# Gating by token block, earlier shared additions and a halved last store in a two-layer transformer kernel

## The chip, the cores and the metric

The kernel runs on one core of a Trainium2 chip, all in 32-bit floats. The metric is the time of one execution on the device in microseconds (us), taken several times; one more execution is recorded by the profiler.

## The reference

Two layers, each of attention and a feed-forward network, on x of shape (2, 512, 1024) and a context of (2, 1024, 1024):

```python
x = x + matmul(fake_quant(layernorm(x)), fake_quant(ctx))        # quantised product
x = x + lora_ffn(layernorm(x))        # x @ W.T + b + 8 routed LoRA experts, routing per batch
x = x + cross_attention(layernorm(x), ctx, ctx)   # 32 heads of 128, 8 key/value heads, rope
x = x + top1_ffn(layernorm(x))        # the end of the kernel, in full:

def _L1_ffn_ref(x, W_up, gate_w, expert_bias, lora_A, lora_B):
    logits = x_flat @ gate_w.T + expert_bias          # 4 experts
    top1 = jnp.argmax(logits, axis=-1)
    one_hot = jax.nn.one_hot(top1, E)
    base_out = jnp.einsum('bth,oh->bto', x, W_up)
    z = jnp.einsum('nh,erh->ner', x_flat, lora_A)     # rank 8
    d = jnp.einsum('ner,ehr->neh', z, lora_B) * SCALE
    delta = jnp.einsum('neh,ne->nh', d, one_hot)
    return base_out + delta.reshape(B, T, H)
```

## The kernel before

**Tiles.** Tokens lie in four blocks (t = 0 to 3) of 128 per batch; `rows(b, t)` is one of them, 128x1024, in SBUF. A map of 1024 to 1024 over 512 tokens is done as a product of 2x2 blocks with seven products instead of eight. `linear(b, ...)` (L562) is such a map; it works in two halves, `blocks(0)` and `blocks(1)`, woven by `pair`. `blocks(s)` gives the token blocks s and 2 + s. Each of the seven products is 16 or 20 TensorE instructions of 128x512 (L347, four or five pairs, each 32-bit product as four instructions) into a bank of PSUM.

**The seven products.** `seven_onto` (L304) adds their results onto rows that are already there. In `linear` their order is 1, 2, 6, 7, 5, 4, 3. Product 1 is copied by ScalarE into `u` (L315); product 6 is added to `u` by VectorE (L317): this is the shared sum. Each other product is added by VectorE onto its quarter `c` of the rows (L320), and for the products 5, 4 and 3 GpSimd then adds `u` onto that quarter (L322). Products 7 and 4 share a bank, as do 1 and 2, and 5 and 3: the second is accumulated onto the first. The output projection of the attention uses `seven_onto` with its own order. `linear` is called for the first network of both batches (L1076) and for the last network of both batches (L1203 and L1238), which is the end of the kernel.

**The gates.** `gated` is the choice of the expert in the last network. It makes, for each token block, 16 TensorE instructions (L937; eight fp32 products of 128x36: 4 logits and 4 x 8 ranks) into one PSUM tile `gaccs` of four parts. Then, for each block, seven VectorE operations choose the expert: bias (L949), maximum (L951), equality (L953), a preference for the first (L954), maximum (L955), equality (L956), and the product of the chosen expert's mask with the ranks, out of PSUM into `z` (L961). Two blocks share a tile `z2`, which GpSimd sets to zero first (L959). TensorE transposes each block's `z` (L971), VectorE copies the result to `zT` (L972) and takes a difference (`split_tokens`). `zT` is the LoRA operand of the final map.

**The order.** `gated` is a generator; whoever calls `next` places its parts. For batch 0 this happens in the attention's loop, where TensorE, VectorE, ScalarE and GpSimd all keep the order in which the program names their instructions. `hooks` maps (head, phase) to calls: at (61, 2) `begin_map` creates the generator; at (62, 1) `advance(last["gates"], 4)` issues the products of all four blocks; at (62, 2) the VectorE and GpSimd operations follow; at (63, 1) the transposes, and the final map begins. Around them stand the sums of the attention's denominators (four transposes L712, a reduction L714, a reciprocal L785), the exponentials of the last head (L794 on VectorE, L797 on ScalarE, L800, L803, L804 and L805 on GpSimd), the last product of a head with its values (L811), and the normalisation L822 on GpSimd.

For batch 1 `turned_and_gated` is woven with the final map of batch 0: one step of it after each product. Each step turns a block of normalised rows (L204, copies L205 and L206) and issues a block's gate products. TensorE keeps the order of the program there too; on the other engines a scheduler sets the order.

**The end.** The rows of batch 1 are stored by four transfers of 512 KB on SyncE's queue (L1244); the last map's products 4 and 3 write the last quarters.

Of the kernel before, what the change touches and what calls it, by code (L numbers as in the profile page):

```python
# [15 lines left out]
ALU = mybir.AluOpType  # L16
AX = mybir.AxisListType

P = 128
# [5 lines left out]
E1, R1 = 4, 8  # L25
# [6 lines left out]
NT = S // P  # L32
NC = D // P
NKT = S2 // P
HALF = 512
# [4 lines left out]
def decoder_kernel(  # L40
# [25 lines left out]
    nc = tc.nc  # L66
# [8 lines left out]
    def new(shape, tag, bufs, dtype=F32):  # L75
        n_tiles[0] += 1
        return sb.tile(list(shape), dtype, tag=tag, name=f"{tag}_{n_tiles[0]}", bufs=bufs)
# [7 lines left out]
    def u2(shape, dtype=F32):  # L85
        return new(shape, "u2", 10, dtype)

    def small(shape):
        return new(shape, "small", 16)

    def ps_wide():
        n_tiles[0] += 1
        return ps.tile([P, D], F32, tag="wide", name=f"wide_{n_tiles[0]}", bufs=2)

    def ps_b(shape=(P, HALF), dtype=F32):
        n_tiles[0] += 1
        return ps.tile(list(shape), dtype, tag="b", name=f"b_{n_tiles[0]}", bufs=4)

    def ps_tr():
        return ps_b((P, 4, P))  # L100
# [16 lines left out]
    for name, ap in qparams.items():  # L117
        t = const.tile([P, 1], F32, name=f"qp_{name}")
        nc.gpsimd.dma_start(t, ap.partition_broadcast(P))
        qp[name] = t  # L120
    for side in ("x1", "x2"):
        t = const.tile([P, 1], F32, name=f"qp_inv_{side}")
# [21 lines left out]
    NGA = E1 + E1 * R1  # L144
# [156 lines left out]
                emit(0, 1, u)  # L301
            yield

    def seven_onto(product, place, order=(1, 6, 2, 7, 5, 4, 3)):  # L304

        banks = {}
        for i in order:
            first = {2: 1, 4: 7, 3: 5}.get(i, i)
            if i == first:
                banks[i] = ps_b()  # L310
            acc = banks[first]
            product(i, acc, i == first)
            if i == 1:
                u = u2([P, HALF])
                nc.scalar.copy(u, acc)  # L315
            elif i == 6:
                nc.vector.tensor_tensor(u, u, acc, ALU.add)  # L317
            else:
                c = place(*{2: (0, 0), 7: (1, 1), 5: (1, 1), 4: (1, 0), 3: (0, 1)}[i])
                nc.vector.tensor_tensor(c, c, acc, ALU.add)  # L320
                if i != 2 and i != 7:
                    nc.gpsimd.tensor_tensor(c, c, u, ALU.add)  # L322
            yield

    def pair(a, b):

        for _ in range(2):
            next(a)
            yield
            next(b)  # L330
            yield
        yield from a
        yield from b
# [11 lines left out]
    def accumulate(acc, pairs, start):  # L345
        for k, (lhsT, rhs) in enumerate(pairs):
            nc.tensor.matmul(  # L347
                acc,
                lhsT,
                rhs,  # L350
                start=start and k == 0,
                stop=k == len(pairs) - 1,
                skip_group_check=True,
            )
# [16 lines left out]
    def rows(b, t):  # L371
        return x[b][t // 2][:, t % 2, :]
# [168 lines left out]
    def chunk(quarters, c, t):  # L541
        return quarters[t // 2][c // 4][:, c % 4, ts(t % 2, P)]
# [19 lines left out]
    def linear(b, h_ops, w_ops, tT, bl):  # L562

        def blocks(s):
            lora = {2: (0, 0), 4: (1, 0), 5: (1, 1), 3: (2, 1)}

            def product(i, acc, start):
                pairs = [
                    (h_ops[i - 1][:, c, ts(s, P)], w_ops(i, c))
                    for c in range(4)  # L570
                ]
                if i in lora:
                    th, nh = lora[i]
                    pairs.append((tT()[th][:, ts(s, P)], bl[:, ts(nh, HALF)]))
                accumulate(acc, pairs, start)

            return seven_onto(
                product,
                lambda i, j: rows(b, 2 * i + s)[:, ts(j, HALF)],
                (1, 2, 6, 7, 5, 4, 3),  # L580
            )

        return pair(blocks(0), blocks(1))

    def split_tokens(tT, diff):
        nc.vector.tensor_tensor(diff, tT[:, 0:256], tT[:, 256:S], ALU.subtract)
        return tT[:, 0:256], tT[:, 256:S], diff
# [236 lines left out]
    def projection(b, o_ops, w_ops):  # L824

        for s in range(2):
            def product(i, acc, start):
                accumulate(
                    acc,
                    [(o_ops[i - 1][:, h, ts(s, P)], w_ops[i][:, h, :]) for h in range(2)],  # L830
                    start,
                )

            yield from seven_onto(product, lambda i, j: rows(b, 2 * i + s)[:, ts(j, HALF)])
# [95 lines left out]
    def gated(quarters):  # L930


        zT, diff = u2([P, S]), u2([P, 256])
        gaccs = ps_wide().rearrange("p (t n) -> p t n", t=NT)
        for t in range(NT):
            for c in range(NC):
                nc.tensor.matmul(  # L937
                    gaccs[:, t, :NGA],
                    chunk(quarters, c, t),
                    ga_t[:, c, :],  # L940
                    start=(c == 0),
                    stop=(c == NC - 1),
                )
            yield
        zs = []
        for t in range(NT):
            gacc = gaccs[:, t, :]
            lg = small([P, E1])
            nc.vector.tensor_tensor(lg, gacc[:, :E1], eb_t, ALU.add)  # L949
            mx = small([P, 1])  # L950
            nc.vector.tensor_reduce(mx, lg, AX.X, ALU.max)  # L951

            nc.vector.tensor_scalar(lg, lg, mx, None, ALU.is_equal)  # L953
            nc.vector.tensor_tensor(lg, lg, prefer, ALU.mult)  # L954
            nc.vector.tensor_reduce(mx, lg, AX.X, ALU.max)  # L955
            nc.vector.tensor_scalar(lg, lg, mx, None, ALU.is_equal)  # L956
            if t % 2 == 0:
                z2 = u2([P, 2, P])
                nc.gpsimd.memset(z2, 0.0)  # L959
            z = z2[:, t % 2]  # L960
            nc.vector.tensor_tensor(  # L961
                z[:, : E1 * R1].rearrange("p (e r) -> p e r", r=R1),
                gacc[:, E1:NGA].rearrange("p (e r) -> p e r", r=R1),
                lg.unsqueeze(2).to_broadcast([P, E1, R1]),
                ALU.mult,
            )
            zs.append(z)
        yield
        tr = ps_tr()
        for t, z in enumerate(zs):  # L970
            nc.tensor.transpose(tr[:, t, :], z, ident)  # L971
        nc.vector.tensor_copy(zT, tr.rearrange("p t n -> p (t n)"))  # L972
        yield split_tokens(zT, diff)
# [150 lines left out]
    last = {"zT": [None] * B, "w": [None] * 7, "h": [None] * 7}  # L1124
# [22 lines left out]
    def fetch_weight(i, ch, nh):  # L1147
        t = last["w"][i - 1] = u8([P, 4, HALF])
        nc.sync.dma_start(
            t,  # L1150
            wupT[ts(ch, 4 * P), ts(nh, HALF)].rearrange("(c p) n -> p c n", p=P),
        )
# [6 lines left out]
    def begin_map():  # L1159
        hs = last["hs"]  # L1160
        last["h"][:2] = hs[0]
        last["gates"] = gated(hs)

    hooks = {(42, 0): [lambda: next(stats)], (42, 1): [turn_away]}
    for t in range(NT):
        hooks[(38 + t, 1)] = [lambda: next(stats)]
    for i in range(2):
# [7 lines left out]
        lambda: fetch_weight(2, 1, 0),  # L1175
        fetch_rows,
        begin_map,
    ]
    hooks[(62, 1)] = [lambda: advance(last["gates"], 4)]
    hooks[(62, 2)] = [  # L1180
        lambda: next(last["gates"]),
        lambda: fetch_weight(7, 0, 1),
        lambda: fetch_weight(3, 1, 1),
    ]
# [28 lines left out]
    for _ in steps:  # L1213
        pass
    hs, norms = normed(1, u4, 4)
    gates = gated(hs)

    def turned_and_gated():
        next(norms)
        yield  # L1220
        next(norms)
        yield
        for _ in range(3):
            next(norms)
            next(gates)
            yield
        next(gates)
        yield
        next(gates)
        yield  # L1230

    side = turned_and_gated()
    weave(main, side, 1)
    for _ in side:
# [5 lines left out]
    zTs[1] = next(gates)  # L1240
    for _ in main:
        pass
    for t in range(NT):
        nc.sync.dma_start(out[1, ts(t, P), :], rows(1, t))  # L1244


def rope_tables():
# [68 lines left out]
```

## Time and profile before

| | us |
|---|---|
| median of 3 runs | 2494.17 |
| lowest and highest | 2492.08, 2495.93 |
| profiled execution, its own time | 2491.89 |
| profiled execution, span from first to last instruction | 2490.1 |
| TensorE busy in the span | 2434.2 |
| VectorE, GpSimd, ScalarE busy | 1852.5, 1011.8, 527.9 |
| mean granted TensorE clock | 0.992 |

In the profile PE is TensorE's products, PEld its loads of weights, DVE VectorE, ACT ScalarE, POOL GpSimd and SP SyncE; SPq is SyncE's DMA queue. L322 is line 322 of the program above. A line of the timeline gives the start and duration in us, engine, line, operation, output and inputs with their shapes, the count, and in brackets the idle time ahead of it with what ended it. A line of the chain that ended last gives start, duration, and the engine or queue on which the end of the span depended then. The busy share of TensorE, 98%, is a mean over stages: the first few slices of the span and a few stretches between stages are less full.

### The profile page before, as it was taken

What the parts mean: (1) busy time and instruction counts of PE and PEld (TensorE: products, weight loads), DVE (VectorE), ACT (ScalarE), POOL (GpSimd) and SP (SyncE); (2) the same over time, 40 slices, a digit from 0 to 9 for tenths busy, and PEclk for the clock granted to TensorE, in tenths of its full rate; (3) what the DMA queues carried; (4) which work ended last, traced back from release to release, by engine and by line L of the source; (5) the groups of instructions that cost most, each with busy time, mean ns of one, the idle gap of its engine ahead of it and who ended that gap; (6) DMA issues with size and microseconds to landing.
All of it is one profiled execution on the core that took longest, in us unless ns stands there. A gap on an engine that the chain in (4) does not pass through costs nothing.

```text
span 2490.1 us, 19684 instructions
## 1 busy us (share of the span) xinstructions
PE 2434.2 (98%) x6848; PEld 1214.5 (49%) x6856; DVE 1852.5 (74%) x2036; ACT 527.9 (21%) x615; POOL 1011.8 (41%) x536
## 2 busy tenths in 40 slices
PE   7999999999999998989999999999999999999999
PEld 3477458654444443434444444444444444445454
DVE  5848774345886557988888888888898888887552
ACT  1201221011222222232222222222222222222100
POOL 0000010111000001557676767676777676667421
PEclk8999999999999999999999999999999999999999
DMA  7225233012895221343323322442334233323301
GB/s 264 103 92 204 75 124 106 26 68 106 283 329 199 76 93 47 102 131 107 84 80 109 109 83 80 138 150 79 114 106 130 62 104 114 104 74 110 127 26 43
DMA packets 148243, 283.83 MB, mean 114 GB/s; under 512 B 29296, under 2 KB 47232, under 8 KB 146352
## 3 DMA queue, kind: packets, MB, share of 16 engines
q1 hardware_dynamic: 107888, 242.25, 28.7%
q10 hardware_dynamic: 39824, 39.60, 6.6%
q8 instruction: 55, 0.90, 0.2%
q0 software_dynamic: 432, 0.71, 0.1%
q14 instruction: 44, 0.36, 0.0%
HBM read 221.44 MB, written 61.08 MB: 113 GB/s over the span
## 4 chain that ended last, share of the span: by engine, by line
PE 59%; DVE 7%; POOL 2%; issue 2%; DMA 1%; ACT 1%; SPq 0%; POOLq 0%; DVEq 0%; ACTq 0%
PE b L347 26%; PE wide L748 15%; PE b L811 15%; PE wide L712 2%; DVE u L794 2%; DMA u<-in_wo_dram 1%; PE wide L937 1%; DVE u L772 1%; DVE u L774 1%; DVE small L714 1%; POOL u L804 1%; POOL u L803 0%; DVE u L762 0%; DVE u L222 0%; DVE u L219 0%
## 5 line engine op out<-in xcount | busy, mean ns | idle before, releaser
L347 PE MATMUL b<-u,u 128*128 128x512 f32 (+1 forms) x3648 | 1408.6, 543 | 25.3 <-DVE u L291 10.8
L347 PEld LDWEIGHTS b<-u,u 128*128 128x128 f32 x3648 | 691.4, 191 | 707.5 <-issue 619.4
L748 PE MATMUL wide<-u,u 128*128 128x512 f32 x1024 | 456.9, 597 | 15.7 <-DVE small L714 8.5
L811 PE MATMUL b<-u,u 128*128 128x512 f32 x1024 | 461.2, 593 | 0.0
L800 POOL TENSOR_TENSOR u<-u 128x1024 f32<-128x1024 f32 x64 | 151.6, 2369 | 747.4 <-DMA row<-small 385.0
L762 DVE TENSOR_TENSOR u<-wide,u 128x1024 f32<-128x1024 f32 x256 | 312.7, 1224 | 128.2 <-PE wide L748 127.8
L797 ACT ACTIVATE u<-u 128x2048 f32<-128x2048 f32 x128 | 244.6, 1911 | 675.7 <-DVE u L794 626.4
L748 PEld LDWEIGHTS wide<-u,u 128*128 128x128 f32 x1024 | 193.4, 191 | 268.0 <-issue 176.8
L794 DVE TENSOR_TENSOR u<-u,b 128x2048 f32<-128x2048 f32 x128 | 290.0, 2266 | 0.0
L811 PEld LDWEIGHTS b<-u,u 128*128 128x128 f32 x1024 | 186.7, 192 | 185.2 <-issue 185.2
L322 POOL TENSOR_TENSOR u<-u,u 128x512 f32<-128x512 f32 x120 | 189.4, 1599 | 195.0 <-DVE u L320 175.4
L320 DVE TENSOR_TENSOR u<-u,b 128x512 f32<-128x512 f32 x200 | 135.7, 679 | 135.1 <-PE b L347 135.1
L803 POOL TENSOR_TENSOR u<-u,u 128x1024 f32<-128x1024 f32 x64 | 150.8, 2356 | 35.6 <-ACT u L797 34.6
L804 POOL TENSOR_TENSOR u<-u,u 128x1024 f32<-128x1024 f32 x64 | 151.9, 2374 | 5.0
L822 POOL TENSOR_TENSOR u<-u,u 128x512 f32<-128x512 f32 x64 | 119.9, 1873 | 21.4 <-DMA u<-row 21.4
L1053 POOL DMA_DIRECT2D u<-in_b_dram x1 | 0.6, 558 | 301.8 <-PE wide L450 301.8
L216 ACT ACTIVATE u<-u 64x512 f32<-64x512 f32 x72 | 45.2, 628 | 344.6 <-DVE u L293 167.3
L712 PEld LDWEIGHTS wide<-ident,u 128*128 128x128 f32 x512 | 80.2, 204 | 64.6 <-issue 54.7
L770 DVE TENSOR_TENSOR u<-u 128x1024 f32<-128x1024 f32 x64 | 111.4, 1741 | 0.0
L772 DVE TENSOR_TENSOR u<-u,u 128x1024 f32<-128x1024 f32 x64 | 106.3, 1660 | 0.2
L805 POOL TENSOR_TENSOR u<-u 128x512 f32<-128x512 f32 x64 | 102.0, 1594 | 5.0
L774 DVE TENSOR_TENSOR u<-u,u 128x1024 f32<-128x1024 f32 x64 | 97.4, 1522 | 0.2
(125 smaller groups left out, 1552.3 us busy)
## 6 DMA issues: line engine op xcount, KB each, us to landing
u<-row ACTq DMA_DIRECT2D x128, 256.0 KB, 3.7
u<-wo SPq DMA_DIRECT2D x64, 512.0 KB, 4.0
u<-in_wo_dram SPq DMA_DIRECT2D x48, 512.0 KB, 4.5
u<-in_wq_dram SPq DMA_DIRECT2D x32, 512.0 KB, 4.0
q<-u SPq DMA_DIRECT2D x64, 256.0 KB, 2.1
u<-in_wo_dram SPq DMA_DIRECT2D x16, 1024.0 KB, 8.1
wo<-u SPq DMA_DIRECT2D x32, 512.0 KB, 3.7
u<-q SPq DMA_DIRECT2D x64, 256.0 KB, 4.1
```

The source lines that it names most:

```text
L320: nc.vector.tensor_tensor(c, c, acc, ALU.add)
L322: nc.gpsimd.tensor_tensor(c, c, u, ALU.add)
L347: nc.tensor.matmul(acc, lhsT, rhs, start=start and k == 0, stop=k == len(pairs) - 1, skip_group_check=True,)
L748: nc.tensor.matmul(sc[:, ts(n, HALF)], self.kT[:, ts(2 * j + n, P)], self.qT, start=True, stop=True,)
L762: nc.vector.tensor_tensor(self.e[j // 2][:, js, :], sc.rearrange("p (k q) -> p k q", k=2), mask[j], ALU.add)
L772: nc.vector.tensor_tensor(m, m, e[1][:, 0:2, :], ALU.max)
L794: nc.vector.tensor_tensor(e, e, self.nmf.unsqueeze(1).to_broadcast([P, 4, S]), ALU.add)
L797: nc.scalar.activation(e, e, AF.Exp)
L800: nc.gpsimd.tensor_tensor(d, e[:, 0:2, :], e[:, 2:4, :], ALU.add)
L803: nc.gpsimd.tensor_tensor(d, d, e[:, 0:2, :], ALU.add)
L804: nc.gpsimd.tensor_tensor(d, d, e[:, 2:4, :], ALU.add)
L811: nc.tensor.matmul(self.acc, self.v[:, k, :], self.e[j][:, k % 4, :], start=(k == 0), stop=(k == NKT - 1),)
```

## The change

There are three parts. In `gated` both tiles `z2` are created and set to zero in a first step of the generator, which `begin_map` (batch 0) and a `next(gates)` ahead of the second step of the normalisation (batch 1) now take; each token block's VectorE operations are issued directly behind its gate products, in the same step; the step that held them all is gone, with its `next` at (62, 2). In `seven_onto` an option `u_first`, set by `linear`, issues the three GpSimd additions of `u` as soon as `u` holds product 6, ahead of VectorE's additions of the products 7, 5, 4 and 3. The rows of batch 1 are stored in the order 0, 2, 3, 1, and block 1 in two transfers of 128x512.

```diff
                 emit(0, 1, u)
             yield
 
-    def seven_onto(product, place, order=(1, 6, 2, 7, 5, 4, 3)):
+    def seven_onto(product, place, order=(1, 6, 2, 7, 5, 4, 3), u_first=False):
 
         banks = {}
+        places = {2: (0, 0), 7: (1, 1), 5: (1, 1), 4: (1, 0), 3: (0, 1)}
+
+        def add(c, what):
+            nc.gpsimd.tensor_tensor(c, c, what, ALU.add)
+
         for i in order:
             first = {2: 1, 4: 7, 3: 5}.get(i, i)
             if i == first:
...
                 nc.scalar.copy(u, acc)
             elif i == 6:
                 nc.vector.tensor_tensor(u, u, acc, ALU.add)
+                if u_first:
+                    for k in (5, 4, 3):
+                        add(place(*places[k]), u)
             else:
-                c = place(*{2: (0, 0), 7: (1, 1), 5: (1, 1), 4: (1, 0), 3: (0, 1)}[i])
+                c = place(*places[i])
                 nc.vector.tensor_tensor(c, c, acc, ALU.add)
-                if i != 2 and i != 7:
-                    nc.gpsimd.tensor_tensor(c, c, u, ALU.add)
+                if i != 2 and i != 7 and not u_first:
+                    add(c, u)
             yield
 
     def pair(a, b):
...
                 product,
                 lambda i, j: rows(b, 2 * i + s)[:, ts(j, HALF)],
                 (1, 2, 6, 7, 5, 4, 3),
+                True,
             )
 
         return pair(blocks(0), blocks(1))
...
 
 
         zT, diff = u2([P, S]), u2([P, 256])
+        zs = []
+        for _ in range(2):
+            z2 = u2([P, 2, P])
+            nc.gpsimd.memset(z2, 0.0)
+            zs += [z2[:, 0], z2[:, 1]]
+        yield
         gaccs = ps_wide().rearrange("p (t n) -> p t n", t=NT)
         for t in range(NT):
+            gacc = gaccs[:, t, :]
             for c in range(NC):
                 nc.tensor.matmul(
-                    gaccs[:, t, :NGA],
+                    gacc[:, :NGA],
                     chunk(quarters, c, t),
                     ga_t[:, c, :],
                     start=(c == 0),
                     stop=(c == NC - 1),
                 )
-            yield
-        zs = []
-        for t in range(NT):
-            gacc = gaccs[:, t, :]
             lg = small([P, E1])
             nc.vector.tensor_tensor(lg, gacc[:, :E1], eb_t, ALU.add)
             mx = small([P, 1])
...
             nc.vector.tensor_tensor(lg, lg, prefer, ALU.mult)
             nc.vector.tensor_reduce(mx, lg, AX.X, ALU.max)
             nc.vector.tensor_scalar(lg, lg, mx, None, ALU.is_equal)
-            if t % 2 == 0:
-                z2 = u2([P, 2, P])
-                nc.gpsimd.memset(z2, 0.0)
-            z = z2[:, t % 2]
             nc.vector.tensor_tensor(
-                z[:, : E1 * R1].rearrange("p (e r) -> p e r", r=R1),
+                zs[t][:, : E1 * R1].rearrange("p (e r) -> p e r", r=R1),
                 gacc[:, E1:NGA].rearrange("p (e r) -> p e r", r=R1),
                 lg.unsqueeze(2).to_broadcast([P, E1, R1]),
                 ALU.mult,
             )
-            zs.append(z)
-        yield
+            yield
         tr = ps_tr()
         for t, z in enumerate(zs):
             nc.tensor.transpose(tr[:, t, :], z, ident)
...
         hs = last["hs"]
         last["h"][:2] = hs[0]
         last["gates"] = gated(hs)
+        next(last["gates"])
 
     hooks = {(42, 0): [lambda: next(stats)], (42, 1): [turn_away]}
     for t in range(NT):
...
     ]
     hooks[(62, 1)] = [lambda: advance(last["gates"], 4)]
     hooks[(62, 2)] = [
-        lambda: next(last["gates"]),
         lambda: fetch_weight(7, 0, 1),
         lambda: fetch_weight(3, 1, 1),
     ]
...
 
     def turned_and_gated():
         next(norms)
+        next(gates)
         yield
         next(norms)
         yield
...
             next(norms)
             next(gates)
             yield
-        next(gates)
-        yield
         next(gates)
         yield
 
...
     zTs[1] = next(gates)
     for _ in main:
         pass
-    for t in range(NT):
+
+    for t in (0, 2, 3):
         nc.sync.dma_start(out[1, ts(t, P), :], rows(1, t))
+    for i in range(2):
+        nc.sync.dma_start(out[1, ts(1, P), ts(i, HALF)], rows(1, 1)[:, ts(i, HALF)])
 
 
 def rope_tables():
```

## Prediction

> **What bounds the kernel now.** I read the page first, then the chain that ended last, TensorE's timeline and clock around the gate stretches, the waits there, and the end of the span.
>
> ```profile
> PE 2434.2 (98%) x6848; PEld 1214.5 (49%) x6856; DVE 1852.5 (74%) x2036; ACT 527.9 (21%) x615; POOL 1011.8 (41%) x536
> PE 59%; DVE 7%; POOL 2%; issue 2%; DMA 1%; ACT 1%; SPq 0%; POOLq 0%; DVEq 0%; ACTq 0%
> L322 POOL TENSOR_TENSOR u<-u,u 128x512 f32<-128x512 f32 x120 | 189.4, 1599 | 195.0 <-DVE u L320 175.4
> ```
>
> TensorE is busy 98% of the span, so outside its few stalls only its idle time, its clock and the last few microseconds can change. The chain shows the stretch between the last two heads, where batch 0's gates are made; the timeline below it shows where TensorE then stands still.
>
> ```profile
> 2293.29 9.03 PE wide L937 x64
> 2302.32 0.90 PE wide L712 x4
> 2303.22 7.78 PE b L811 x16
> ```
> ```profile
> 2317.45 0.33 PE L971 MATMUL b<-ident,u 128*128 128x128 f32 x1 [1.31 <-DVE u L961]
> 2319.61 0.47 PE L971 MATMUL b<-ident,u 128*128 128x128 f32 x1 [1.83 <-DVE u L961]
> 2321.07 0.48 PE L971 MATMUL b<-ident,u 128*128 128x128 f32 x1 [0.98 <-DVE u L961]
> 2322.47 0.47 PE L971 MATMUL b<-ident,u 128*128 128x128 f32 x1 [0.93 <-DVE u L961]
> ```
>
> The four transposes wait for the selection of the four token blocks, 5.05 us of idle TensorE. The clock costs as much again (steps of the span: busy time of PE, its weight loads, VectorE, ScalarE, GpSimd, each with its count, then granted clock, DMA share, GB/s):
>
> ```profile
> 2294.66:2298.07 3.41, 3.41 (x33) 3.41 (x33) 0.00 (x0) 0.59 (x1) 3.41 (x3) 1.00 0.41 79
> 2298.07:2301.48 3.41, 3.41 (x18) 3.41 (x18) 0.00 (x0) 0.00 (x0) 2.73 (x3) 0.50 0.00 0
> 2315.13:2318.55 3.42, 1.34 (x4) 0.32 (x2) 1.28 (x4) 0.00 (x0) 3.34 (x5) 1.00 1.04 399
> 2318.55:2321.96 3.41, 0.95 (x2) 0.36 (x2) 2.83 (x18) 0.00 (x0) 0.10 (x1) 0.50 1.03 409
> ```
>
> In this trace the clock moves in steps of 3.41 us: a step full of the small gate products (128x36) is followed by half rate, and so is one that is mostly idle (1.34 busy); a step full of 128x512 products brings it back (half rate ends at 2304.90 and at 2325.37).
>
> **Batch 0's gates: the sum before.** From 2293.29 to the end of the 16 products behind the transposes (2331.08) 37.79 us pass. At full clock the work is 64 gate products, 4 x 1.71 (the rows of batch 1, `2403.94 1.71`) = 6.84; L712 0.47; L811 6.87; 12 products of L347 5.16; four transposes 0.44 (batch 1's row); 16 products 6.87: 26.65. So 11.14 us are lost: 5.05 of stalls, the rest half clock.
>
> **What the change moves there.** The zeros leave the path: L961 no longer waits 4.02 us for the memset L959, and each block's seven VectorE operations come behind its gate products, so by the time of the transposes they are long done. If that were all, the transposes would follow the twelve products at 2316.14 at full clock: stalls −5.05, and about 1.3 us of single transposes at half rate (4 x 0.36), with the products after them: 2322.94 − 2316.59 = 6.35 to the end of the transposes, and 8.14 − 6.87 = 1.27 behind them, −7.62.
>
> But the built program shows a wait that the diff does not: all four blocks' sums lie in one PSUM tile (`gaccs`), and now VectorE reads block t before TensorE writes block t+1. The gate products of blocks 1, 2 and 3 wait for L961 of the block before, in both batches. Queued behind a waiting gate product is all of TensorE's later work. TensorE's order itself is the same in both programs, so nothing fills these waits in batch 0, where the 64 stood together. The chain from L949 to L961 takes
>
> ```profile
> 2319.47 0.15 DVE L949 TENSOR_TENSOR small<-wide,eb_t 128x4 f32<-128x4 f32 x1
> ...
> 2320.82 0.19 DVE L961 TENSOR_TENSOR u<-wide,small 128x32 f32<-128x32 f32 x1
> ```
>
> and TensorE restarts at 2321.07: 1.60 us (1.54 for the next block). That is the price of a stall when VectorE is alone. It is not: L953 and L956 are 0.23 us alone, but 1.91 and 2.01 where GpSimd runs L800 and L803; both end with GpSimd's operation (2310.72, 2313.16).
>
> ```profile
> 2308.83 1.91 DVE L953 TENSOR_SCALAR small<-small,small 128x4 f32<-128x4 f32 x1
> 2311.17 2.01 DVE L956 TENSOR_SCALAR small<-small,small 128x4 f32<-128x4 f32 x1
> ```
>
> GpSimd is busy in the new place: L805 to 2295.90, both memsets (0.56), L822 1.26, three L322 3.72, so until 2301.4. Block 0's L953 is held about 0.3 us by L805; block 1's L953 and L956 by the L322s, each by 0 to 1.2. Stalls: 3 x 1.54 + 0.3 = 4.9 at the least, 7.2 at most; I take 6.1.
>
> Half clock: the step 2294.67 to 2298.07 now holds fewer gate products than before, so half rate starts at 2298.07 as before. The blocks: t=0 ends 2295.00, t=1 runs 2296.9 to 2299.2, t=2 from about 2302.3, t=3 ends near 2310.7 (3.42 each at half rate, 1.6 and up to 3.1 between); only the next step that is full of large products restores the clock, at 2315.13 on this grid, or 2311.72 if the steps fall kindly. Work done at half rate loses its own full-clock length: some 6.0 us in the first case, 4.3 in the second. Lost: 6.1 + 6.0 or 4.3 = 12.1 or 10.4, against 11.14; ends 4.9 + 3.6 and 7.2 + 7.7. I take +0.5 (−2.6 to +3.8): what the transposes no longer wait, the gates do. The transposes themselves then wait for nothing: block 3's chain runs beside L712 and L811.
>
> A rule speaks otherwise. The Trainium skill, "TensorE: Matmul & The Clock Gate", section "What's actually happening", has the clock halve after at least one idle window of about 3.4 us. The row from 2294.66 differs: that step had no idle at all, and half rate followed. By the rule none of these stalls would halve the clock, and the stretch would lose its stalls alone.
>
> VectorE's 28 operations are moved past L714, L785 and L794 of head 63; VectorE stands idle there until 2303.26, waiting for L712. These come as much later as TensorE's L712, and with them ScalarE's and GpSimd's work up to L805 (2316.92), whose reader, L712 at 2330.92, has 14 us to spare.
>
> **Batch 1's gates.** Each block's 16 gate products are separated by 4.4 to 5.2 us of other TensorE work for t=1 and t=2 (`2405.65 3.51` and 0.87 of L204), more than the 1.6 us chain, with up to 2.8 left for held operations. Not for t=3: its gates stand right behind product 4, and in VectorE's new order L320 of product 4 stands inside the chain of t=2, ahead of L956 and L961. Product 4 ends at 2423.07; L320 0.69, L956 0.23, L961 0.19 and hand-overs bring 2424.3: a stall of 1.2 us. Before, the clock stood at 1.00 throughout. A step with 1.2 us idle and 1.71 of gate products may halve the next: 1.7 us, at even odds 0.85. Sum +2.05 (0 to +2.9). Nothing is gained: the transposes at 2436.01 did not wait.
>
> **The early shared additions.** 24 L322 (four calls, two blocks, three each) move ahead of L320 of products 7, 5, 4 and 3; the number stays. In the first network TensorE has no gap there, and in the final maps the first addition ends about 1.3 us before product 7 does (u ready 2358.09, addition done 2359.4, product 7's L320 2360.78; the tightest pair, 576.14, has 0.1). I take 0; if one were late, the L320 that frees the bank has 4.3 us of the next product before TensorE asks for it.
>
> **The tail.**
>
> ```profile
> 2484.56 0.69 DVE L320 TENSOR_TENSOR u<-u,b 128x512 f32<-128x512 f32 x1 [3.60 <-PE b L347]
> 2485.32 1.26 POOL L322 TENSOR_TENSOR u<-u,u 128x512 f32<-128x512 f32 x1 [3.02 <-DVE u L320]
> 2486.61 0.33 SPq L1244 DMA_DIRECT2D out_dram<-u  x1
> ```
>
> The last L322 goes: −1.33 (2485.32 to 2486.61, and the hand-over). The last store is 256 KB instead of 512 KB: rows of 256 KB land in 2.1 (q), 2.0 (kT), 2.4 (v), the old store in 2.6; 2.1 as median of 64: −0.5. One more store on SP costs nothing: the queue idles there. −1.83 (−1.5 to −1.9).
>
> **Sum.** +0.5 + 2.05 − 1.83 = +0.7 on the profiled execution, 2491.89 (span 2490.1 and 1.79 around it), which lies 2.28 under the median of the three runs, inside their spread. Put on the median, 2494.9. Its own range: −2.6 + 0 − 1.9 = −4.5 to +3.8 + 2.9 − 1.5 = +5.2, 2489.7 to 2499.4. A measurement of this kernel can tell about 0.2%, 5 us.
>
> **The rivals.** (A) Faster: the new waits cost little, because the clock is not halved in the gate stretch. Then the stretch loses 4.9 to 6.1 instead of 11.14, −6.2 to −5.0; with batch 1 at +1.2 or 0 and the tail −1.83, −8.1 to −5.6. With no wait at all, −7.62 − 1.83 = −9.45. For it: the large idle goes. Against it: 64 gate products without any gap already halve the clock. 2484.7 to 2488.6; chance 0.16. (B) Slower: half rate spreads. Each further step of 3.41 us full of work costs 1.71; with the stalls at 7.2, two steps more in batch 0 (+3.8 + 1.7) and two in batch 1 (1.2 + 3.4) less 1.5 of tail it is +8.6. It decides where the stalls reach 7.2 and seven steps run at half clock, against before's four (five in batch 0, two in batch 1: 7.2 + 6.0 − 11.14 + 1.2 + 3.4 − 1.8 = +4.9). For it: the gates alternate with idle, both of which lower the clock here. Against it: 16 large products behind them restore it. 2499.4 to 2502.8; chance 0.21. (C) Only the tail moves: VectorE is quick, the waits and the old stalls cancel and batch 1's stall is hidden, 2492.3; chance 0.10. My forecast has 0.53.
>
> **How the numbers follow.** A is faster by over 0.2%, B slower; forecast and C lie within, but for a sliver: 0.16, 0.63, 0.21. The range takes in forecast and C, and reaches halfway into B and some four tenths into A, which leaves out about 0.1 on either side: 2487.0 to 2501.0.
>
> **What would show it.** Right: TensorE waits at L937 three times in batch 0 (1.6 to 3.1 us each, released by VectorE's selection) and once in batch 1 (about 1.2), no waits of the transposes, half clock from about 2298 to 2312 or 2315, none near 2320, and the last store behind VectorE's addition. Wrong: clock 1.00 through the gates (A), clock 0.50 anywhere in batch 1's stretch for two steps (B), or L937 without waits.

## The result and the profile after

Over ten executions each the changed kernel took 2499.28 us in the median (2493.53 to 2503.69), the kernel before 2493.73 (2490.43 to 2498.84). The ratio is 1.0021, with an interval of 1.0011 to 1.0030: slower by 5.2 us (2.7 to 7.5), where 0.7 was forecast, and just past the 0.2% that the prediction took as the least that a measurement of this kernel can tell. A second series of the same kernel, beside other experiments, gave 1.0018 (1.0009 to 1.0026). So it is a small loss, and a real one.

The page of the profile after, its first line of busy times and the line of GpSimd's shared additions (L322 is now L310):

```profile
PE 2438.3 (98%) x6848; PEld 1216.8 (49%) x6856; DVE 1852.9 (74%) x2036; ACT 527.7 (21%) x615; POOL 1010.5 (41%) x536
```
```profile
L310 POOL TENSOR_TENSOR u<-u,u 128x512 f32<-128x512 f32 x120 | 186.4, 1579 | 185.0 <-DVE u L322 161.9
```

The instruction counts are the same. TensorE is busy 4 us longer with them, but most of that lies where the profiles of all the kernels differ: 2.8 us ahead of the gates (2244.20 instead of 2241.38 up to the last product of head 61 with its values). Only 1.1 lie in batch 0's gate stretch (48.02 instead of 46.94) and 0.2 in batch 1's. The mean granted clock over the whole span was even a little higher, 0.994 instead of 0.992. The profiled execution (2493.53, span 2491.8) was the shortest of the ten, and up to the gates it ran 2.0 us ahead of before's profile. That part differs by up to 7.6 us between single profiles of all the kernels here (2283.82 to 2291.45 at the last product of head 61 with its values), so I compare from that product on. The four stretches in us, each read from the timeline of one execution, from the start of one product to the start of the next one named; "end" is the end of the span, which is given to 0.1 us, so that the last column and the sums are good to about 0.05:

| kernel | to head 63's last product | to batch 1's first turn (L204) | to the last product | to the end | sum against before |
|---|---|---|---|---|---|
| before | 51.99 | 60.76 | 85.34 | 6.17 | 0 |
| changed | 55.46 | 60.76 | 86.96 | 4.80 | +3.72 |
| changed_again | 55.18 | 60.76 | 86.96 | 4.72 | +3.36 |

Batch 0's gates lost 3.47 us, batch 1's 1.62, and the end gained 1.4. TensorE's timeline in batch 0, with the line numbers of the new program (L937 is now L953, L961 is L969, L712 is L721, L811 is L820, L971 is L978):

```profile
2291.12 1.87 PE L953 MATMUL wide<-ga_t,u 128*128 128x36 f32 x16
2297.19 3.63 PE L953 MATMUL wide<-ga_t,u 128*128 128x36 f32 x16 [4.20 <-DVE u L969]
2302.41 3.63 PE L953 MATMUL wide<-ga_t,u 128*128 128x36 f32 x16 [1.59 <-DVE u L969]
2307.69 3.63 PE L953 MATMUL wide<-ga_t,u 128*128 128x36 f32 x16 [1.65 <-DVE u L969]
...
2325.07 0.60 PE L978 MATMUL b<-ident,u 128*128 128x128 f32 x4
```

The four waits of the transposes are gone, and three waits of the gate products, 7.44 us, stand in their place, each released by the selection of the block before. The last three blocks take 3.63 instead of 1.87: half clock. In the clock's steps of 3.41 us, with the columns that the prediction explains (granted clock is the last figure but two):

```profile
2293.62:2297.03 3.41, 0.00 (x0) 0.00 (x0) 3.21 (x5) 0.59 (x1) 3.41 (x6) 1.00 0.28 59
2297.03:2300.44 3.41, 3.25 (x16) 3.25 (x16) 0.10 (x1) 0.00 (x0) 2.24 (x2) 0.50 0.02 5
...
2307.27:2310.69 3.42, 3.00 (x14) 3.00 (x15) 0.27 (x2) 0.00 (x0) 0.00 (x0) 0.50 0.00 0
2310.69:2314.10 3.41, 3.41 (x10) 2.33 (x11) 2.50 (x10) 0.00 (x0) 0.00 (x0) 0.50 0.00 0
2314.10:2317.50 3.40, 3.40 (x9) 1.48 (x8) 3.40 (x2) 1.63 (x1) 0.00 (x0) 1.00 0.14 24
```

A step without any product is followed by five steps at half clock. The fifth, from 2310.69, is full of products, though only 2.1 us of it are large ones (L820 starts at 2312.01), and it ends the half clock. Why the first wait is so long stands in VectorE's and GpSimd's timelines, side by side:

```profile
2293.41 0.98 DVE L965 TENSOR_SCALAR small<-small,small 128x4 f32<-128x4 f32 x1
2294.43 1.19 DVE L966 TENSOR_TENSOR small<-small,prefer 128x4 f32<-128x4 f32 x1
2295.66 0.16 DVE L967 TENSOR_REDUCE small<-small 128x1 f32<-128x4 f32 x1
2295.85 1.00 DVE L968 TENSOR_SCALAR small<-small,small 128x4 f32<-128x4 f32 x1
```
```profile
2293.82 0.56 POOL L946 MEMSET u<- 128x256 f32 x2
2294.34 1.26 POOL L831 TENSOR_TENSOR u<-u,u 128x512 f32<-128x512 f32 x1
2295.56 3.71 POOL L310 TENSOR_TENSOR u<-u,u 128x512 f32<-128x512 f32 x3
```

L965 ends with the memsets (2294.39 and 2294.38), L966 with L831 (2295.62 and 2295.60), L968 with the first of the three L310: 3.17 us where block 1's chain, with GpSimd idle, has 0.23 + 0.16 + 0.23. In batch 1 there is one wait, before block 3, and VectorE's rows ahead of it show what it waits for:

```profile
2425.90 1.95 PE L953 MATMUL wide<-ga_t,u 128*128 128x36 f32 x16 [1.39 <-DVE u L969]
```
```profile
2423.51 1.23 DVE L253 TENSOR_TENSOR u<-u,u 128x1024 f32<-128x1024 f32 x1
2424.65 0.15 DVE L967 TENSOR_REDUCE small<-small 128x1 f32<-128x4 f32 x1
2424.72 0.68 DVE L328 TENSOR_TENSOR u<-u,b 128x512 f32<-128x512 f32 x1
2425.31 0.22 DVE L968 TENSOR_SCALAR small<-small,small 128x4 f32<-128x4 f32 x1
2425.57 0.19 DVE L969 TENSOR_TENSOR u<-wide,small 128x32 f32<-128x32 f32 x1
```

L967, L968 and L969 are the end of block 2's selection. The addition of product 4 (L328) stands inside it, and so do three operations of the normalisation (L245, L248 and L253, 1.2 us each).

And the end:

```profile
2487.70 0.69 DVE L328 TENSOR_TENSOR u<-u,b 128x512 f32<-128x512 f32 x1 [3.61 <-PE b L355]
2488.41 0.33 SPq L1253 DMA_DIRECT2D out_dram<-u  x1
```

The last store now follows VectorE's addition at once (L320 is now L328).

### The profile page after: what moved, and what is told of

It is laid out like the page before. It is cut to its first block, busy times and chain, and to the rows that moved or that the text cites. A ratio compares the mean times of both kernels' runs of the same rounds, so it can differ in the third digit from the quotient of the medians.

```text
span 2491.8 us, 19716 instructions
## 1 busy us (share of the span) xinstructions
PE 2438.3 (98%) x6848; PEld 1216.8 (49%) x6856; DVE 1852.9 (74%) x2036; ACT 527.7 (21%) x615; POOL 1010.5 (41%) x536
## 4 chain that ended last, share of the span: by engine, by line
PE 72%; DVE 8%; POOL 2%; issue 2%; DMA 1%; ACT 1%; SPq 0%; ACTq 0%; DVEq 0%; POOLq 0%
PE b L355 38%; PE wide L757 15%; PE b L820 15%; PE wide L721 2%; DVE u L803 2%; PE wide L204 1%; PE wide L953 1%; DVE u L771 1%; DMA u<-in_wo_dram 1%; POOL u L812 1%; POOL u L813 1%; PE b L645 1%; DVE u L222 1%; DVE u L781 1%; DVE u L219 0%
## 5 line engine op out<-in xcount | busy, mean ns | idle before, releaser
L820 PE MATMUL b<-u,u 128*128 128x512 f32 x1024 | 461.4, 594 | 0.0
L803 DVE TENSOR_TENSOR u<-u,b 128x2048 f32<-128x2048 f32 x128 | 290.2, 2268 | 0.0
L820 PEld LDWEIGHTS b<-u,u 128*128 128x128 f32 x1024 | 186.7, 192 | 185.2 <-issue 185.2
L310 POOL TENSOR_TENSOR u<-u,u 128x512 f32<-128x512 f32 x120 | 186.4, 1579 | 185.0 <-DVE u L322 161.9
L328 DVE TENSOR_TENSOR u<-u,b 128x512 f32<-128x512 f32 x200 | 135.9, 680 | 136.5 <-PE b L355 136.5
L812 POOL TENSOR_TENSOR u<-u,u 128x1024 f32<-128x1024 f32 x64 | 150.7, 2355 | 36.6 <-ACT u L806 36.4
L831 POOL TENSOR_TENSOR u<-u,u 128x512 f32<-128x512 f32 x64 | 119.9, 1874 | 14.8 <-DMA u<-row 14.8
L721 PEld LDWEIGHTS wide<-ident,u 128*128 128x128 f32 x512 | 80.1, 204 | 64.2 <-issue 55.5
L814 POOL TENSOR_TENSOR u<-u 128x512 f32<-128x512 f32 x64 | 102.0, 1594 | 5.0
```

Of the source, the lines that this page charges most:

```text
L310: nc.gpsimd.tensor_tensor(c, c, what, ALU.add)
L803: nc.vector.tensor_tensor(e, e, self.nmf.unsqueeze(1).to_broadcast([P, 4, S]), ALU.add)
L812: nc.gpsimd.tensor_tensor(d, d, e[:, 0:2, :], ALU.add)
L820: nc.tensor.matmul(self.acc, self.v[:, k, :], self.e[j][:, k % 4, :], start=(k == 0), stop=(k == NKT - 1),)
```

## The experiments

Each ratio is to the kernel before on the same chip. "Sum" is the sum of the four stretches against before.

**1. The gating alone.** `seven_onto` and the last stores as before.

```diff
                 (1, 2, 6, 7, 5, 4, 3),
-                True,
             )
...
-    for t in (0, 2, 3):
+    for t in range(NT):
         nc.sync.dma_start(out[1, ts(t, P), :], rows(1, t))
-    for i in range(2):
-        nc.sync.dma_start(out[1, ts(1, P), ts(i, HALF)], rows(1, 1)[:, ts(i, HALF)])
```

> Only the gating part of the change; shared additions and last stores as before. Theory W (the gate products now wait for VectorE's selection, and the stretch runs at half clock): batch 0's stretch +3.5 us against before, with waits at the gate products of 4.2, 1.6 and 1.6 us, five steps at half clock; batch 1's +1.6 with one wait of 1.4; together +5.1 us, ratio 1.0020. Theory P (the early shared additions on GpSimd disturb VectorE and cost the time, the gating is neutral): within 1 us of before.

Measured: 1.0033 (1.0021 to 1.0045), +8.2 us; sum +5.10 (55.44, 60.76, 86.96, 6.20); waits of 4.21, 1.59, 1.65 and 1.39, five steps at half clock. P falls: the loss is all in the gating. The profile gives the expected 5.1 us to a tenth, just under the interval (5.2 to 11.2).

**2. The rest alone.** `gated`, its hooks and `turned_and_gated` as before, the rest as changed: the diff of the change without its middle part.

> Only the early shared additions and the halved last store; gating as before. Theory W: the last stretch alone moves, -1.3 us for the GpSimd addition and -0.4 for the smaller transfer, -1.7 us, ratio 0.9993; the waits of the four transposes (5 us) stay. Theory P: slower than before by 3 us or more, ratio 1.0012 or above.

Measured: 0.9999 (0.9990 to 1.0008), sum −1.33 (52.06, 60.76, 85.33, 4.78). The whole of it lies in the last stretch; in the stretches traced here the early additions move nothing. The −0.4 that W gave the smaller transfer did not come. The measurement can't tell −1.3 us from nothing.

**3. The choice behind all four blocks.** The products of the four blocks stand together again, and their selection follows them at once.

```diff
                     stop=(c == NC - 1),
                 )
+            yield
+        for t in range(NT):
+            gacc = gaccs[:, t, :]
             lg = small([P, E1])
...
-            yield
+        yield
         tr = ps_tr()
...
-    hooks[(62, 1)] = [lambda: advance(last["gates"], 4)]
+    hooks[(62, 1)] = [lambda: advance(last["gates"], 5)]
```

> The change, but all four blocks' gate products stand together again and the selection of all four follows at once on VectorE (ahead of the next head's reduction), the zeros early. Theory W: no gate product waits and no transpose waits; the first half-clock steps stay (64 small products in a row), the second pair at the transposes goes: -7 us in batch 0, 0 in batch 1, -1.7 at the end: -8.7 us, ratio 0.9965. Rival H (the small products and the clock set the stretch, not the waits): the stretch stays half clocked to its end as in the changed kernel, within 3 us of before.

Measured: 0.9981 (0.9972 to 0.9990), −4.7 us; sum −2.10 (51.30, 60.76, 85.34, 4.76). No gate product waits, as W says, and batch 1 is back at 85.34. But batch 0 gained 0.7 instead of 7, because of a wait that no theory had, the half-clock step behind it, and a third half-clock step in the gates (2294.79 to 2305.03; before had two there):

```profile
2317.82 2.96 PE L355 MATMUL b<-u,u 128*128 128x512 f32 x4 [3.36 <-ACT u L320]
```

The chain that ended last shows where it comes from: VectorE's 28 operations are now ahead of the last head's reduction, which starts at 2308.07, 5 us behind the end of the transposes that it reads (L721).

```profile
2308.07 0.69 DVE small L723
2308.79 0.19 DVE small L794
2309.00 5.44 DMA row<-small
2314.46 0.34 ACTq L736
```

On ScalarE's queue L736 waits for that transfer, behind it stand the second exponential (2314.90, 1.91), a copy, and L320, which empties the bank that TensorE needs. The "14 us to spare" of the prediction were counted to another reader (L712 of the next head). Not all of the wait comes from the edit: the transfer took 5.44 us, where the one at this place takes 1.9 to 2.7 in the eleven other profiles. By my estimate that is 1.5 of the 3.36 us: VectorE's L803, ahead of the second exponential, ended at 2313.33, and in before the exponential starts 0.04 behind the same operation, here at 2314.90. Why the transfer was slow is not shown.

**4. A PSUM tile for each block**, from a pool with two buffers.

```diff
-        gaccs = ps_wide().rearrange("p (t n) -> p t n", t=NT)
         for t in range(NT):
-            gacc = gaccs[:, t, :]
+            gacc = ps_wide()
```

> The change with a PSUM tile for each token block (two buffers taken in turn) in place of one tile for all four. Theory W (the wait comes from the shared tile): block 1's gate products wait for nothing, block 2's for block 0's selection, about 2.5 us, block 3's for nothing; batch 1's stall of 1.4 us goes; half clock one or two steps shorter: 5 to 9 us faster than the changed kernel, -2 to -6 us against before, ratio 0.9976 to 0.9992. Rival H (the stretch is set by the clock that the small products bring): the same time as the changed kernel within 2 us, ratio 1.0010 to 1.0025.

Measured: 0.9983 (0.9975 to 0.9992), −4.2 us; sum −4.72 (48.67, 60.76, 85.34, 4.77), 8.4 under the changed kernel. Blocks 0 and 1 run together, and one wait is left, for the buffer of block 0:

```profile
2292.66 3.66 PE L952 MATMUL wide<-ga_t,u 128*128 128x36 f32 x32
2298.85 7.01 PE L952 MATMUL wide<-ga_t,u 128*128 128x36 f32 x32 [2.53 <-DVE small L960]
```

(The row names L960, which is block 1's first operation; block 0's last, L968, ends at 2298.70, 0.15 us ahead of the product.) Half clock lasts three steps. In batch 1 the wait is gone, with nothing else changed. This shows that the shared tile made the wait, and that the same edit with two buffers is a gain, though not yet the −9.45 that the prediction gave a change without any wait.

**5. The zeros alone**, in the kernel before.

```diff
+        zeros = []
+        for _ in range(2):
+            z2 = u2([P, 2, P])
+            nc.gpsimd.memset(z2, 0.0)
+            zeros.append(z2)
+        yield
         gaccs = ps_wide().rearrange("p (t n) -> p t n", t=NT)
...
-            if t % 2 == 0:
-                z2 = u2([P, 2, P])
-                nc.gpsimd.memset(z2, 0.0)
-            z = z2[:, t % 2]
+            z = zeros[t // 2][:, t % 2]
...
         last["gates"] = gated(hs)
+        next(last["gates"])
```

> The kernel before with one edit: both z tiles are zeroed at (61, 2) (and one step earlier in batch 1); the selection stays after the exponentials of the last head. Theory W: L961 loses its 4.0 us wait for the memset, but its chain then runs beside GpSimd's L803, L804 and L805, each of which holds a VectorE operation with a scalar operand by up to 2.2 us; the transposes, 5.05 us of waits before, keep 1 to 3; half clock about as before: -2 to -4 us, ratio 0.9984 to 0.9992. Rival: the memset was not the cause of the transposes' waits, the VectorE chain is; within 1 us of before.

Measured: 0.9990 (0.9982 to 0.9999), −2.5 us; sum −2.61. The waits of the transposes shrank from 5.05 to 2.68:

```profile
2323.94 0.33 PE L974 MATMUL b<-ident,u 128*128 128x128 f32 x1 [1.60 <-DVE u L964]
2325.34 0.48 PE L974 MATMUL b<-ident,u 128*128 128x128 f32 x1 [1.08 <-DVE u L964]
```

The chain of selections, 5.7 us alone in experiment 3 (2302.33 to 2308.07), took 12 (2313.21 to 2325.28): five of its operations with a scalar operand lasted 0.70 to 2.01, beside GpSimd's sums. W holds, within its range; the measurement's interval (−4.5 to −0.2) would not tell it from the rival's 1 us, but the waits of the transposes do.

**6. Gate blocks apart.** The four blocks at (61, 2), (62, 1), (62, 2) and ahead of the final map's first two products, the transposes behind those.

```diff
         next(last["gates"])
+        next(last["gates"])
...
-    hooks[(62, 1)] = [lambda: advance(last["gates"], 4)]
+    hooks[(62, 1)] = [lambda: next(last["gates"])]
     hooks[(62, 2)] = [
+        lambda: next(last["gates"]),
...
-                zTs = [next(last["gates"]), None]
+                next(last["gates"])
+                zTs = [None, None]
...
                 advance(main, 2)
+                zTs[0] = next(last["gates"])
```

> The changed kernel with batch 0's four gate blocks apart: one at (61, 2), one at (62, 1), one at (62, 2), one ahead of the final map's first products, and the transposes behind those (16 products of 128x512 later). Theory W: a block's selection runs beside 7 to 8 us of large products, no gate product waits for more than 1 us and, as no 3.41 us step is filled by gate products or idle, the clock stays at 1.00: batch 0's stretch loses 0 to 2 us in place of 11 before; batch 1's stall of 1.4 us stays: -9 +1.6 -1.4 = -9 us, ratio 0.9964. Rival H (a block of gate products by itself halves the clock): three or four half-clock steps, -4 us or less.

> The same with a PSUM tile for each token block. Theory W: as spread, without batch 1's stall: -10.5 us against before, ratio 0.9958, 1.6 us under spread. Rival (the stall in batch 1 is hidden by something else and the tile does not matter there): the same as spread within 0.5 us in batch 1's stretch of the trace.

Measured: spread 0.9995 (0.9986 to 1.0004), sum −1.22 (48.82, 60.75, 88.66, 4.81); spread_tiles 0.9971 (0.9959 to 0.9982), sum −4.40 (48.95, 60.76, 85.34, 4.81). Both of W's totals (−9 and −10.5) failed. No gate product of batch 0 waits, but TensorE does in the middle of the projection, and half clock follows for two steps (the rows are spread_tiles'):

```profile
2298.25 5.85 PE L355 MATMUL b<-u,u 128*128 128x512 f32 x8 [5.39 <-DVE u L328]
```
```profile
2297.41 0.19 DVE L968 TENSOR_TENSOR u<-wide,small 128x32 f32<-128x32 f32 x1 [6.24 <-POOL u L946]
2297.52 1.47 DVE L328 TENSOR_TENSOR u<-u,b 128x512 f32<-128x512 f32 x2
```

Block 0's L968 waits for the memsets, which stand on GpSimd behind four sums of head 62 (to 2297.07), and the L328 that frees the projection's bank stands behind L968. The number of H for spread, −4 us or less, fits, but not its reason: the half-clock steps follow steps that were mostly idle (0.79 and 0.50 us busy), not the blocks of gate products. In batch 1, spread's 88.66 holds the wait of 1.39 and, in this one profile, a half-clock step (2422.50 to 2425.91); with a tile per block both are gone.

**7. spread_tiles with the zeros a phase earlier.**

```diff
-        last["gates"] = gated(hs)
         next(last["gates"])
-        next(last["gates"])
+    def begin_gates():
+        last["gates"] = gated(last["hs"])
+        next(last["gates"])
...
+    hooks[(61, 1)] = [begin_gates]
```

> spread_tiles with one edit: the zeros are set at (61, 1), one phase ahead of the first gate block, so that GpSimd's memsets stand in its queue ahead of the sums L809 to L814 of head 62. Theory W: L968 of block 0 no longer waits 6.2 us for the memset, the L328 behind it come in time, and TensorE's 5.4 us wait in the middle of the projection goes, with it the two half-clock steps that follow it: 7 to 8.5 us faster than spread_tiles, -14 us against before if nothing new is late, ratio 0.994 to 0.9955. Rival (the projection waits for VectorE's longer queue, not for the memset): the wait stays above 3 us and the ratio at 0.996 to 0.998.

Measured: 0.9957 (0.9945 to 0.9970), 2483.64 us; sum −10.60 (42.84, 60.75, 85.34, 4.71), 6.2 under spread_tiles. The wait fell from 5.39 to 1.43, and no step between the gates and the last product is at half clock:

```profile
2293.70 3.70 PE L355 MATMUL b<-u,u 128*128 128x512 f32 x8 [1.43 <-DVE u L328]
```
```profile
2284.00:2300.00 16.00, 14.57 (x62) 8.48 (x61) 11.74 (x17) 5.00 (x4) 11.81 (x7) 1.00 0.59 165
2300.00:2330.00 30.00, 30.00 (x101) 15.78 (x100) 20.75 (x33) 6.12 (x7) 10.99 (x7) 1.00 0.67 237
```

What remains of the wait is a selection held by a sum: L967 lasts 2.41 and ends with GpSimd's L812. This kernel beats both, the changed one by some 15 us; W's 7 to 8.5 was too much by that last wait.

**8. Gate blocks apart, but later.** At (62, 1), (62, 2), (63, 1) and behind two products of the final map; the transposes behind head 63's products. Against tile_per_block:

```diff
-    hooks[(62, 1)] = [lambda: advance(last["gates"], 4)]
+    hooks[(62, 1)] = [lambda: next(last["gates"])]
     hooks[(62, 2)] = [
+        lambda: next(last["gates"]),
...
-                zTs = [next(last["gates"]), None]
+                next(last["gates"])
+                zTs = [None, None]
...
                 advance(main, 2)
+                next(last["gates"])
...
     for _ in range(2):
         next(steps)
+    zTs[0] = next(last["gates"])
```

> tile_per_block with the gate blocks at (62, 1), (62, 2), (63, 1) and behind the final map's first two products, the transposes behind the last head's products; the zeros at (61, 2). Theory W: block 0's selection is held about 4 us by GpSimd's L814, L831 and L310 as in the changed kernel and delays the exponentials of the last head, so that TensorE may wait up to 2 us once for ScalarE's copy behind them; otherwise no gate product waits for more than 1 us and at most two steps run at half clock: 5 to 8 us less than before in batch 0, -1.4 at the end, ratio 0.9962 to 0.9975. Rival H (any block of gate products brings half clock): four steps or more at half clock, ratio 0.998 or above.

Measured: 0.9962 (0.9948 to 0.9976), sum −9.60 (43.34, 61.20, 85.34, 4.78): just beyond the −5 to −8 and −1.4 of W, whose wait for ScalarE's copy did not come; TensorE waits once, 0.94 for GpSimd's L814, and one step is at half clock.

```profile
2299.45 1.12 PE L721 MATMUL wide<-ident,u 128*128 128x128 f32 x4 [0.94 <-POOL u L814]
```

H falls here and in experiment 7: a block of gate products alone does not halve the clock. The one step at half clock (2299.30 to 2302.71) follows a step that held a block of gate products, 0.8 us of large products and most of this wait.

**9. The changed kernel again.**

> The changed kernel as it is, for another profile, since the 3.41 us steps of the clock need not fall alike in two executions. Theory W: the same waits (4.2, 1.6, 1.6 and in batch 1 1.4 us); the stretch at half clock five steps, or four or six where the grid falls otherwise (1.7 us each); batch 0 +2 to +5 us against before, in all +3.7, ratio 1.0008 to 1.003. Rival (something outside the gates and the end costs the rest of the measured 5 us): the stretches ahead of 2290 us are over 1.5 us longer than in every profile of the kernels with the old gating.

Measured: 1.0018 (1.0009 to 1.0026), sum +3.36; waits of 4.19, 1.59, 1.65 and 1.39, and again five steps, 17.07 us, at half clock. The stretch ahead of the gates was 2.3 us longer here than in before's profile and 2.0 shorter in the first, and it was longest of all, 2291.45, in a kernel with the old gating (zeros_early): nothing of the change is in it.

## Why the prediction was right, and what it mis-sized

The mechanism was on record: waits of the gate products in place of those of the transposes, in both batches, made by the shared tile, which the diff does not show; half clock through the whole stretch; a gain at the end. Experiments 1, 2 and 4 show each by itself. The total of +0.7 was 3.0 under the profile's +3.7, and the measured median, 5.2 over before, is at the edge of the forecast's own range, 0.1 us from where rival B's begins: the mechanism was the forecast's, but its size was nearly as well foretold by the rival. The terms:

- **Stalls in batch 0**, 6.1 (4.9 to 7.2): 7.44. The end of GpSimd's work, 2301.4, and its hold on VectorE were seen, but put on the wrong block: 0.3 for block 0 and up to 2.4 for block 1. Block 0 was held three times (4.20 against 1.6 alone) and block 1 not at all, because its products, 2.3 us later than forecast and all at half clock, ended when GpSimd was done (2300.86 after 2299.27). I had also left L966 (here `prefer` times the equality) out of the operations that are held.
- **Half clock in batch 0**, 6.0 or 4.3, taken in the middle: five steps in all three profiles of this gating, 7.2 us by the same subtraction (41.26 from the first gate product to the end of the sixteen, less 26.65, less 7.44). The first case, from 2298.07 to 2315.13, was the right one; nothing in the trace of before spoke for the kind grid (steps that fall more favourably) that I averaged in. Nor is the +0.5 the sum of its terms: 6.1 and the middle of 6.0 and 4.3, less 11.14, give +0.1. Together these two terms are the 3 us: +3.47 instead of +0.5.
- **What restores the clock**: the prediction reads from before's trace that a step full of 128x512 products does it. The steps that did were not full of them: they held 1.9 us of L811 ahead of 2304.90 and 2.6 of L347 ahead of 2325.37; in the changed kernel it was 2.1, in changed_again 1.6. A step at half clock with 0.9 us of them (spread_tiles) was followed by another. The five steps of the first case come out the same.
- **Batch 1**, +2.05: +1.62. The wait is 1.39 (1.2 forecast). Product 4's L328 stands inside the chain as argued, and holds L968 back by 0.59 of it; the rest comes from the normalisation's operations in the same chain, which took 5.6 us (2420.18 to 2425.76) instead of 1.6. The half-clock step at even odds came in one of four profiles that have the wait (spread); where it came, the step ahead held 0.93 us of large products, where it didn't (changed), 1.19.
- **The early additions**, 0: 0, with the stretch from head 63 to batch 1 at 60.76 in each of these kernels with and without them. The same holds for the first network: from the turn (L204) at 485.61 to the one at 612.08 before's trace has 126.47 us, and the changed kernel's 126.48 (484.53 to 611.01). The margin of 0.1 that the prediction names at 576.14 is in no row: product 7's L320 starts there at 578.74, 1.3 behind the addition.
- **The end**, −1.83: −1.4 (4.71 to 4.81 in the nine profiles with the new end, 6.16 to 6.20 in the three with the old). The addition was worth 1.27, near the 1.33 forecast. The smaller store brought 0.1 to 0.2 instead of 0.5: from its issue to the end of the span 3.39, before 3.49. It landed in 2.0 (2.2 in the median of both halves) instead of 2.6, but some 0.4 more passed between its landing and the end of the span; why is not shown.
- **What was moved past**: that L805's reader "has 14 us to spare" was true in the changed kernel, where TensorE is late as well. Experiment 3 shows that it was incomplete: ScalarE's copy of the final map's first product stands in the same queue and has less. VectorE's reduction came 4.9 us later and TensorE waited 3.36, 1.5 of it for the slow transfer, which leaves the copy about 3 us to spare (an estimate from these figures).

Rival A needed a clock of 1.00 through the gates; it was 0.50. Rival B needed seven half-clock steps; there were five. Rival C needed batch 1's stall to be hidden; it was 1.39.

On the clock, the Trainium skill ("TensorE: Matmul & The Clock Gate", "What's actually happening") asks for an idle window before half rate. In the changed kernel one step was idle, and rule and row agree. In experiment 3 the step ahead of half rate, nearly all gate products, had no idle, as in before's row:

```profile
2291.38:2294.79 3.41, 3.41 (x31) 3.24 (x30) 0.69 (x1) 0.59 (x1) 3.33 (x5) 1.00 0.30 46
2294.79:2298.20 3.41, 3.41 (x18) 3.41 (x18) 0.00 (x0) 0.59 (x1) 3.41 (x4) 0.50 0.16 38
```

The profile models the ends of products, so short idle times inside such a row would not show; as far as it shows, the measurement decides against the rule as a complete one.

What stays open: for the changed kernel the profiles give +3.4 and +3.7, the medians +4.5 and +5.2, with intervals that hold both; for gate_only, choose_after_four and spread_tiles profile and median differ by 2.6 to 3.1, and the sum lies just outside the interval. One profile shows one execution; half-clock steps that fall otherwise in the others would do it. For the changed kernel and gate_only the granted clocks fit that: the profiled execution has 0.994 and is the shortest, the others have 0.990 to 0.992. For spread_tiles they do not: there the profiled execution has the highest clock, 0.996, and is the longest. In choose_after_four the slow transfer may be part of it. The cause stays open.

## What to carry to other kernels

A consumer set "right behind" its producer costs nothing only if the next producer writes to another tile: look in the built program for the wait that a shared PSUM tile makes, and give neighbouring blocks different buffers (two, taken in turn, left one wait of three here). Before moving work ahead on a queue, list every queue it passes, GpSimd's memset and ScalarE's copies too, and follow each to the next TensorE wait. A handful of small products did best here between large ones, one block at a time: in spread_zeros no gate product waited, and the clock was kept.

## What the runs showed of the hardware

A VectorE product of 128x4 with two operands in SBUF (L966) lasted 1.19 us beside a GpSimd addition, against 0.16 alone, and L965 was held through GpSimd's memsets as well. One trip of 2 KB through DRAM (`row<-small`) took 5.44 us in experiment 3, against a median of 3.0 over the kernel before and 1.9 to 2.7 at the same place in the other profiles, on the path that TensorE waited for. Sixteen gate products in a row, 1.71 us, between large products never halved the clock (spread_zeros); with a wait of 0.94 behind them half clock followed once (spread_late); 64 in a row did it each time.
